# Masked attention and graph convolution over 32 items: the layer norm's steps and the last items' steps placed by hand

## The chip, the core and the metric

The kernel runs on one core of a Trainium2 chip. The metric is the device time of one execution in microseconds (us); before the change it is 2993.8 us, the median of three runs (2991.41 to 2994.5).

## The reference

32 items of 512 nodes with 512 features pass through masked attention with a layer norm, and then through a graph convolution with a layer norm. All arrays are fp32.

```python
q, k, v = (x @ Wq + bq), (x @ Wk + bk), (x @ Wv + bv)        # 8 heads of 64
scores = einsum('bihd,bjhd->bhij', q, k) / 8 + where(adj == 0, -1e9, 0)
x = layernorm(x + einsum('bhij,bjhd->bihd', softmax(scores), v))
norm_adj = adj * deg_inv_sqrt[:, None] * deg_inv_sqrt[None, :]
x = layernorm(x + einsum('nm,bmo->bno', norm_adj, x @ weight) + bias)
```

## The kernel before, in words

**Tiles and products.** Every item is a 512 x 512 matrix. The products with Wv, Wk, Wq and the convolution's weight are split into two by two blocks of 256 and done as seven block products instead of eight (`seven`, L252, and `second`, L590). For that, each weight (`wv`, `wk`, `wq`, `w1`) and the transposed input (`XT`) lies in a tile of seven slots: four blocks and three differences of them. One such product fills one PSUM buffer of the pool `ps_mm`, which has three (L91), so each product can start only when what reads the product three buffers earlier is done. Piece k of `seven` says who reads its product: k = 0 ScalarE (or VectorE, for the values), k = 1 to 6 VectorE. k = 3 is the one that makes `u2`.

**Blocks of attention.** An item's eight heads go in four blocks of two heads. `for k in range(S + 1)` (L686) runs over all 128 blocks of all items (S is 128). In a turn it makes the first half of the scores of block k (`scores`: TensorE, then VectorE's clip and mask, then ScalarE's exponential), the products with the values of block k - 1 (`values`), on every other turn the sums of the exponentials (`sums`), GpSimd's sums over tiles (`accumulate`), and the second half of the scores. Then comes a share of `side`, other work that fills TensorE.

**What sets the order.** Every engine keeps the order in which the program records its instructions (`InOrder`, L34; that is why nearly all rows of the profile have the line L44). `side` is a list of pieces (cost, function, arguments), and `run(side, share)` (L654) takes pieces from its head until their costs reach a share of the rest: a quarter in the first turn of an item, then a third, then a half, then all. A product costs 2.1, the transpose of sums 0.6, and nearly everything else 0. A piece of no cost that stands behind the product at which the share is reached waits for the next turn, behind that turn's attention.

**What side holds.** In item b's turns: the products of values, keys and queries of item b + 1 (`values_of`, `keys_and_queries`, 21 products), the transpose of item b + 2 (`turns`), the attention's layer norm of item b - 1 (`finish`, L448), and the convolution of item b - 1 (`convolve`, L546). `finish` has these steps: `inverse` (transpose of sums and reciprocals), `add` (VectorE multiplies, GpSimd adds the residual), `measure` (VectorE mean and variance), `root` (GpSimd), `judge` (a count for the fallback), `norm` (ScalarE, `hi`), `split` (VectorE `lo`, GpSimd adds the bias), `grow` (ScalarE). Each is done for four row tiles. `convolve` has four products with the adjacency (`first`), four differences (`parts`, GpSimd), seven products with the weight (`second`), and `measure`, `root` and `store`. Before the change, `weave(chain, main[5:])` (L537) spreads the 23 steps of the layer norm evenly over the products that remain.

**The end.** With no later item's products left, the last item's turns take what was held back: the `second` of item 29 (`held`) and all of item 30's convolution but its `second`. After the last turn, item 30's `second` is laid between the steps of item 31's layer norm, and item 31's own convolution follows (`block` in place of `first`, so that it can begin with the first row tile). The residuals of item 31 are loaded into two tiles of the pool `kq`, the exponentials' sums of its blocks into `acc` tiles, parts of `XT` and one `kq` tile, and its attention output into a third use of the two `yT` tiles, which item 29's convolution still reads.

Of the kernel before, what the change touches and what calls it, by code (L numbers as in the profile page):

```python
# [9 lines left out]
F32 = mybir.dt.float32  # L10
# [7 lines left out]
P = 128  # L18
# [31 lines left out]
def unshifted(  # L50
# [29 lines left out]
    B, N, D = x.shape  # L80
    NT = N // P
    DT = D // P
    G = H // 2
# [17 lines left out]
    HALF = N // 2  # L101
# [29 lines left out]
    R = {}  # L131

    def load_residual(b):

        if b < B - 2:
            t = acts.tile([P, NT, D], F32, name="xr", tag="zT", bufs=1)
            R[b] = [t[:, i, :] for i in range(NT)]
        elif b == B - 2:
            R[b] = [XT[:, i].rearrange("p u o -> p (u o)") for i in range(NT)]
        else:  # L140
            t = [acts.tile([P, 2, D], F32, name="xr2", tag="kq", bufs=5) for _ in range(2)]
            R[b] = [t[i // 2][:, i % 2, :] for i in range(NT)]
        for i in range(NT):
            nc.sync.dma_start(R[b][i], x[b, ts(i, P), :])

# [209 lines left out]
    def accumulate(s):  # L355


        b, g, jj = s
        n = 2 * ORDER.index(g) + jj
        a = None  # L360
        if b == B - 1:
            if n in (2, 6, 7):
                a = XT[:, 0:2] if n == 7 else XT[:, 4:6]
                a = a.rearrange("p k u o -> p k (u o)")
            elif n == 3:
                a = acts.tile([P, 2, N], F32, name="acc3", tag="kq", bufs=5)
        if a is None and (jj == 0 or b == B - 1):
            a = work.tile([P, 2, N], F32, name="acc", bufs=2)
        if a is not None:
            ACC.setdefault((b, g), []).append(a)  # L370
            gpsimd.tensor_add(a, E[s][0], E[s][1])
        else:
            for l in range(2):
                gpsimd.tensor_add(ACC[b, g][0], ACC[b, g][0], E[s][l])

    def values(s):

        b, g, jj = s
        e = E.pop(s)
        if jj == 0:  # L380
            AV[b, g] = ps_av.tile([P, N], F32, name="av")
        av = AV[b, g]
        for l in range(2):
            j = 2 * jj + l
            for k in range(2):
                tensor.matmul(
                    av[k * HD : (k + 1) * HD, :], V[b][:, j, ts(2 * g + k, HD)], e[l][:, k, :],
                    start=j == 0, stop=j == NT - 1,
                )
        if jj == 0:  # L390
            return

        yb = work.tile([P, 4, NT, 32], F32, name="yb", bufs=1)
        vector.transpose(
            yb.rearrange("p l i s -> p i l s"), av.rearrange("p (i r l) -> p i l r", i=NT, l=4)
        )
        if g == ORDER[0]:
            YT[b] = acts.tile([P, NT, D], F32, name="yT")  # L400
        for q in range(4):
            nc.sync.dma_start(
                YT[b][:, :, (4 * g + q) * 32 : (4 * g + q + 1) * 32],
                yb[32 * q : 32 * (q + 1)],
            )
# [131 lines left out]
    def weave(side, main):  # L537

        out, done = [], 0
        for k, piece in enumerate(main):  # L540
            due = len(side) * (k + 1) // len(main)
            out += side[done:due] + [piece]
            done = due
        return out + side[done:]

    def convolve(b):  # L546
# [22 lines left out]

        def take(d, p, copy):  # L570
            if d == 0:
                t["z"] = acts.tile([P, 4, 2, HALF], F32, name="zT", bufs=1)
            i, u = divmod(d, 2)
            z = t["z"].rearrange("p (j i) u n -> p j i u n", i=2)
            copy(z[:, :, i, u], p.rearrange("p (j n) -> p j n", j=2))
# [3 lines left out]

        def combine(at):  # L580
            if at == 0:
                t["parts"] = acts.tile([P, 3, 2, HALF], F32, name="parts", tag="hi", bufs=1)
            to, a, c = ((4, 2, 0), (5, 3, 4), (6, 3, 2), (2, 5, 1))[at]
            engine = vector if last and at < 2 else gpsimd
            engine.tensor_tensor(slot(to), slot(a), slot(c), ALU.subtract)
# [100 lines left out]
    for k in range(S + 1):  # L686
        b, at = divmod(k, G)
        if at == 1:
            run(side)
            if b:  # L690
                load_residual(b - 1)
            if b + 2 < B:
                load_x(b + 2, 0)
            if b + 1 < B:
                main, kq = values_of(b + 1) + keys_and_queries(b + 1, 0), keys_and_queries(b + 1, 1)
                turn0, turn1 = turns(b + 2) if b + 2 < B else ([], [])
                main += kq[:2] + turn0 + kq[2:5]
            if b == 0:
                w1_parts = [(0, weigh_part, (w1, gpsimd, i)) for i in range(4)]
                side = main[:7] + [(0, degrees, ())] + weave(w1_parts, main[7:]) + kq[5:] + turn1  # L700
            elif b < B - 1:
                f, c = finish(b - 1), convolve(b - 1)
                norm, split, grow = f["norm"], f["split"], f["grow"]
                chain = f["inverse"] + f["add"] + f["measure"] + f["root"] + f["judge"] + norm[:2] + split[:1]
                chain += norm[2:3] + split[1:2] + norm[3:] + split[2:] + grow
                side = weave(rest, main[:5]) + weave(chain, main[5:])
                side += c["first"] + c["parts"][:2] + kq[5:6] + c["parts"][2:3] + kq[6:] + turn1[:1]
                if b < B - 2:
                    s = c["second"]
                    side += s[:1] + c["parts"][3:] + s[1:3] + turn1[1:2] + s[3:4] + turn1[2:3] + s[4:5] + turn1[3:4]  # L710
                    side += s[5:6] + c["measure"][:1] + turn1[4:] + s[6:] + c["measure"][1:2]
                    rest = c["measure"][2:] + c["root"] + c["store"]
                else:
                    side += c["parts"][3:]
                    held = c
            else:
                f, c = finish(b - 1), convolve(b - 1)
                s, norm, split = held["second"], f["norm"], f["split"]
                side = s[:1] + f["inverse"] + s[1:2] + f["add"][:2] + s[2:3] + f["add"][2:] + s[3:4] + f["measure"][:2]
                side += s[4:5] + f["measure"][2:] + f["root"] + s[5:6] + f["judge"] + held["measure"][:2] + s[6:]  # L720
                spread = norm[:2] + held["measure"][2:3] + split[:1] + norm[2:3] + held["measure"][3:] + split[1:2]
                spread += held["root"] + norm[3:] + split[2:] + held["store"]
                side += [(0.5, *piece[1:]) for piece in spread] + c["first"] + c["parts"] + f["grow"]


        if k < S:
            scores((*blocks[k], 0))
        if k:
            values((*blocks[k - 1], 0))
            values((*blocks[k - 1], 1))  # L730
            if k % 2 == 0:
                sums(blocks[k - 1][0], (k - 1) % G // 2)
        if k < S:
            accumulate((*blocks[k], 0))
            scores((*blocks[k], 1))
            accumulate((*blocks[k], 1))
        if k == 0:
            run(two)
        if k == S - 2:
            load_residual(B - 1)  # L740
            last = finish(B - 1)
        if k == S - 1:
            run(last["early"])
        run(side, 1.0 / (G - (at - 1) % G))

    f, e = last, convolve(B - 1)
    s, norm, split, block, add = c["second"], f["norm"], f["split"], e["block"], f["late"][1:]
    run(s[:2] + f["late"][:1] + add[:2] + s[2:3] + add[2:] + s[3:4] + f["measure"] + f["root"] + s[4:5])
    run(norm[:2] + s[5:6] + split[:1] + block[:1] + norm[2:3] + split[1:2] + s[6:] + block[1:2])
    run(norm[3:] + split[2:3] + block[2:3] + split[3:] + block[3:] + f["judge"])  # L750

# [8 lines left out]
    vector.tensor_add(count, count, more)  # L762
    vector.memset(ones, 1.0)

    run(e["unload"] + e["parts"] + f["grow"])
    s, tail = e["second"], c["measure"] + c["root"] + c["store"]
    run(s[:1] + tail[:1] + s[1:2] + tail[1:2] + s[2:3] + tail[2:3] + s[3:4] + tail[3:5] + s[4:5])
    p = ps_mm.tile([1, 1], F32, name="mm")
    tensor.matmul(p, count, ones, start=True, stop=True)
    vector.tensor_scalar(bad, p, -1.0, float(P * B * NT * H + N), op0=ALU.mult, op1=ALU.add)  # L770
    run(s[5:6] + e["measure"][:2] + e["roots"][:1] + tail[5:7] + s[6:] + e["measure"][2:] + e["roots"][1:])
    run(e["stores"][:2] + tail[7:] + e["stores"][2:])
    return nc.values_load(bad, min_val=0, max_val=P * B * NT * H + N * N + N)


# [280 lines left out]
```

## Time and profile before

| what | before |
|---|---|
| median of three runs | 2993.8 us |
| span of the profiled execution | 2990.2 us |
| TensorE busy | 2880.3 us, 96% |
| VectorE busy | 1982.2 us, 66% |
| GpSimd busy | 1807.1 us, 60% |
| ScalarE busy | 1062.9 us, 36% |
| DMA, of 16 engines' span on the main queue | 19.6% |

The page names engines PE (TensorE's matmuls), PEld (its weight loads), DVE (VectorE), ACT (ScalarE), POOL (GpSimd) and SP (the engine that issues most transfers). In a row of the timeline the first number is the start in us, the second the length, "x4" how many instructions were merged into the row, and the bracket at the end the idle time ahead of it with the instruction that ended it. An fp32 matmul of the program shows as two records, so one block product of four matmuls of 256 columns shows as eight records, for keys and queries as a row of 4 with wk and one of 4 with wq. The length of a product is read from one start to the next: 1.73 us without a stall (for instance the key products at 1446.11 and 1447.84).

### The profile page before, as it was taken

How to read it: one execution, taken by the hardware profiler on the slowest of the kernel's cores; microseconds unless marked ns; L12 is line 12 of the kernel's file. 1: busy time of each engine (PE TensorE's matmuls, PEld its weight loads, DVE VectorE, ACT ScalarE, POOL GpSimd, SP SyncE). 2: the span in 40 equal slices, each digit the busy share in tenths (PEclk: the TensorE clock that was granted, in tenths of full speed). 3: DMA queues.
4: the chain of work that ended last, by engine and by line, in shares of the span. 5: the costliest groups of instructions: out<-in, count | busy, mean ns of one | idle time of the engine just before them, and what ended most of it. 6: DMA issues, size and time to landing. Idle time of an engine off the chain costs nothing. (4 is left out here: it accounts for less than half of the span.)

```text
span 2990.2 us, 35412 instructions
## 1 busy us (share of the span) xinstructions
PE 2880.3 (96%) x12966; PEld 1879.2 (63%) x12966; DVE 1982.2 (66%) x2908; ACT 1062.9 (36%) x1342; POOL 1807.1 (60%) x1141
## 2 busy tenths in 40 slices
PE   7999999999999999999999999999999999999987
PEld 5666666666666666666666666666666666666644
DVE  7666766666666667666666666676666766666765
ACT  1234323343333343333433333433334333333333
POOL 3655666656666556666566665566665666655654
PEclk9999999999999999999999999999999999999998
DMA  5111222112121112221121211122211212111111
GB/s 130 29 25 46 50 53 53 39 38 51 46 56 40 39 46 50 53 53 39 36 54 46 55 41 39 46 49 54 53 40 36 53 46 54 43 39 46 46 39 47
DMA packets 383398, 142.40 MB, mean 48 GB/s; under 512 B 280048, under 2 KB 349680, under 8 KB 383216
## 3 DMA queue, kind: packets, MB, share of 16 engines
q1 hardware_dynamic: 381920, 138.75, 19.6%
q8 instruction: 104, 1.70, 0.3%
q10 hardware_dynamic: 1296, 1.31, 0.2%
q14 instruction: 78, 0.64, 0.1%
HBM read 72.88 MB, written 33.55 MB: 36 GB/s over the span
## 5 line engine op out<-in xcount | busy, mean ns | idle before, releaser
L44 ACT ACTIVATE e<-e 128x1024 f32<-128x1024 f32 x512 | 541.2, 1057 | 1056.5 <-DVE e L44 966.2
L44 POOL TENSOR_TENSOR acc<-acc,e 128x1024 f32<-128x1024 f32 x248 | 620.0, 2500 | 158.1 <-ACT e L44 148.2
L44 DVE SCALAR_TENSOR_TENSOR e<-sc,maskT 128x1024 f32<-128x1024 f32 x512 | 601.9, 1217 | 120.3 <-PE sc L44 120.2
L44 POOL TENSOR_TENSOR acc<-e 128x1024 f32<-128x1024 f32 x129 | 303.3, 2351 | 557.9 <-PE mm L44 312.4
L44 PE MATMUL sc<-kq 64*128 64x512 f32 x2048 | 511.1, 617 | 7.9 <-DVE e L44 7.9
L44 PE MATMUL mm<-xT,wk 128*128 128x256 f32 x1792 | 472.9, 387 | 31.7 <-DVE u L44 29.5
L44 PE MATMUL av<-e,v 128*64 128x512 f32 x2048 | 469.8, 601 | 0.0
L44 PE MATMUL mm<-xT,wq 128*128 128x256 f32 x1792 | 459.9, 379 | 0.0
L44 PEld LDWEIGHTS mm<-xT,wk 128*128 128x128 f32 x1792 | 330.5, 190 | 153.9 <-issue 69.0
L44 PE MATMUL mm<-wv,xT 128*128 128x256 f32 x1792 | 402.8, 382 | 15.3 <-DMA wv<-in_L_gnn_Wv_dram 9.4
L44 PEld LDWEIGHTS mm<-wv,xT 128*128 128x128 f32 x1792 | 336.7, 191 | 83.5 <-issue 26.6
L44 PEld LDWEIGHTS mm<-xT,wq 128*128 128x128 f32 x1792 | 341.0, 190 | 45.4
L44 PEld LDWEIGHTS sc<-kq 64*128 64x128 f32 x2048 | 176.8, 186 | 278.1 <-issue 213.2
L44 PEld LDWEIGHTS av<-e,v 128*64 128x64 f32 x2048 | 136.1, 137 | 317.8 <-issue 315.7
L44 POOL TENSOR_TENSOR yT<-yT,xr 128x512 f32<-128x512 f32 (+1 forms) x128 | 180.7, 1431 | 137.4 <-DVE yT L44 128.5
L44 DVE STREAM_TRANSPOSE yb<-av 128x512 f32<-128x512 f32 x128 | 91.7, 717 | 224.9 <-PE av L44 217.2
L44 DVE TENSOR_TENSOR kq<-u,mm 128x512 f32<-128x512 f32 x128 | 87.7, 685 | 220.7 <-PE mm L44 217.1
L44 PE MATMUL mm<-w,zT 128*128 128x256 f32 x1024 | 232.4, 380 | 0.6 <-DVE zT L44 0.6
L44 POOL TENSOR_TENSOR yT<-yT,b_r 128x512 f32<-128x512 f32 x128 | 163.6, 1288 | 100.2 <-DVE lo L44 99.5
L44 PEld LDWEIGHTS mm<-w,zT 128*128 128x128 f32 x1024 | 194.3, 190 | 28.7 <-issue 1.5
L44 PE MATMUL mm<-adjT,hi 128*128 128x512 f32 x496 | 200.4, 404 | 7.6 <-DVE e L44 7.6
L44 PE MATMUL mm<-adjT,lo 128*128 128x512 f32 x496 | 197.6, 398 | 8.3 <-DVE lo L44 8.3
(103 smaller groups left out, 3044.9 us busy)
## 6 DMA issues: line engine op xcount, KB each, us to landing
x<-in_x_dram SPq DMA_DIRECT2D x256, 128.0 KB, 2.9
yT<-yb SPq DMA_DIRECT2D x512, 64.0 KB, 2.4
out_dram<-y SPq DMA_DIRECT2D x128, 256.0 KB, 2.1
xr<-in_x_dram SPq DMA_DIRECT2D x124, 256.0 KB, 3.6
wv<-in_L_gnn_Wv_dram ACTq DMA_DIRECT2D x8, 128.0 KB, 4.7
wk<-in_L_gnn_Wk_dram SPq DMA_DIRECT2D x8, 128.0 KB, 4.1
wq<-in_L_gnn_Wq_dram SPq DMA_DIRECT2D x8, 128.0 KB, 4.7
yT<-in_adj_dram SPq DMA_DIRECT2D x1, 1024.0 KB, 6.7
```

The source lines that it names most:

```text
L44: return self.tc.keep_in_program_order(op(*args, **kwargs))
```

## The change

It moves steps and changes where tiles of the last items lie. It adds no arithmetic and takes none away.

- **Middle items.** `weave` for the layer norm is replaced by a table `beside`, which names for each product of `main` by its number what follows it: the previous convolution's `measure`, `root` and `store` beside products 0 to 7, `inverse` after product 5 (it was between products 4 and 5), two `add` after 6 and two after 7, `measure` after 9, 10 and 11, `judge` after 12, `norm` and `split` after 13 to 17, and the transpose of item b + 2 after 18 (it was after 15). All four `parts` and all four `grow` follow `first`, ahead of the last two key products; two of the `parts` came after them, and `grow` was in the chain before `first`. It is there to keep a step of the layer norm from being held by the attention between two turns.
- **Last turns.** A dictionary `ending` names what each of the last turns takes: three, two and two of the seven held products of item 29 with item 30's layer norm between them. Item 30's four `first` products go behind the last turn, between the steps of item 31's layer norm, and its `second` is spread over those steps, with two products kept for the time of `unload`.
- **Tiles of the last items.** Item 31's residuals go to four slots of `wk`, its sums to pairs of slots of `wq`, `wk`, `wv` and `XT`, its attention output to `wv`, its `zT` and `parts` to `XT`: all are tiles that no later product reads. Its residuals are loaded at the start of turn S - 2 instead of the end.

```diff
-        elif b == B - 2:
-            R[b] = [XT[:, i].rearrange("p u o -> p (u o)") for i in range(NT)]
         else:
-            t = [acts.tile([P, 2, D], F32, name="xr2", tag="kq", bufs=5) for _ in range(2)]
-            R[b] = [t[i // 2][:, i % 2, :] for i in range(NT)]
+            t = XT if b == B - 2 else wk
+            R[b] = [t[:, i].rearrange("p u o -> p (u o)") for i in range(NT)]
...
-            if n in (2, 6, 7):
-                a = XT[:, 0:2] if n == 7 else XT[:, 4:6]
-                a = a.rearrange("p k u o -> p k (u o)")
-            elif n == 3:
-                a = acts.tile([P, 2, N], F32, name="acc3", tag="kq", bufs=5)
+            if n > 1:
+                t, at = ((wq, 0), (wq, 2), (wq, 4), (wk, 4), (wv, 4), (XT, 4))[n - 2]
+                a = t[:, at : at + 2].rearrange("p k u o -> p k (u o)")
...
-            YT[b] = acts.tile([P, NT, D], F32, name="yT")
+            if b < B - 1:
+                YT[b] = acts.tile([P, NT, D], F32, name="yT")
+            else:
+                YT[b] = wv[:, :NT].rearrange("p k u o -> p k (u o)")
...
-                main += kq[:2] + turn0 + kq[2:5]
+                main += kq[:5]
...
-                chain = f["inverse"] + f["add"] + f["measure"] + f["root"] + f["judge"] + norm[:2] + split[:1]
-                chain += norm[2:3] + split[1:2] + norm[3:] + split[2:] + grow
-                side = weave(rest, main[:5]) + weave(chain, main[5:])
-                side += c["first"] + c["parts"][:2] + kq[5:6] + c["parts"][2:3] + kq[6:] + turn1[:1]
+                beside = {
+                    0: rest[:1], 1: rest[1:2], 2: rest[2:3], 4: rest[3:4], 5: rest[4:5] + f["inverse"],
+                    6: rest[5:6] + add[:2], 7: rest[6:] + add[2:], 9: measure[:2], 10: measure[2:3],
+                    11: measure[3:] + f["root"], 12: f["judge"], 13: norm[:2], 14: norm[2:3] + split[:1],
+                    15: norm[3:] + split[1:2], 16: split[2:3], 17: split[3:], 18: turn0,
+                }
+                side = sum(([piece] + beside.get(i, []) for i, piece in enumerate(main)), [])
+                side += c["first"] + c["parts"] + grow + kq[5:] + turn1[:1]
...
+                ending = {
+                    S - 3: s[:1] + f["inverse"] + s[1:2] + add[:2] + s[2:3] + add[2:],
+                    S - 2: s[3:4] + f["measure"][:2] + s[6:] + f["measure"][2:] + f["root"] + f["judge"],
+                    S - 1: s[4:5] + norm[:3] + split[:1] + s[5:6] + norm[3:] + split[1:],
+                    S: [],
+                }
...
-    run(s[:2] + f["late"][:1] + add[:2] + s[2:3] + add[2:] + s[3:4] + f["measure"] + f["root"] + s[4:5])
-    run(norm[:2] + s[5:6] + split[:1] + block[:1] + norm[2:3] + split[1:2] + s[6:] + block[1:2])
-    run(norm[3:] + split[2:3] + block[2:3] + split[3:] + block[3:] + f["judge"])
+    run(first[:1] + end["late"][:1] + add[:2] + first[1:2] + add[2:] + first[2:3] + end["measure"][:2] + first[3:])
+    run(end["measure"][2:] + end["root"] + c["parts"] + f["grow"] + held["measure"] + s[:1] + norm[:1] + s[1:2])
+    run(norm[1:2] + split[:1] + s[2:3] + block[:1] + norm[2:3] + split[1:2] + s[3:4] + block[1:2] + norm[3:])
+    run(split[2:3] + s[4:5] + block[2:3] + split[3:] + block[3:] + e["unload"] + e["parts"] + s[5:] + end["grow"])
```

More of the change, by code (lines that the diff above doesn't have):

```diff
@@ L571, in take @@
             if d == 0:
-                t["z"] = acts.tile([P, 4, 2, HALF], F32, name="zT", bufs=1)
+                t["z"] = XT[:, :4] if last else acts.tile([P, 4, 2, HALF], F32, name="zT", bufs=1)
             i, u = divmod(d, 2)
@@ L581, in combine @@
             if at == 0:
-                t["parts"] = acts.tile([P, 3, 2, HALF], F32, name="parts", tag="hi", bufs=1)
+                t["parts"] = XT[:, 4:] if last else acts.tile([P, 3, 2, HALF], F32, name="parts", tag="hi", bufs=1)
             to, a, c = ((4, 2, 0), (5, 3, 4), (6, 3, 2), (2, 5, 1))[at]
@@ L696, in unshifted @@
                 turn0, turn1 = turns(b + 2) if b + 2 < B else ([], [])
-                main += kq[:2] + turn0 + kq[2:5]
+                main += kq[:5]
             if b == 0:
                 w1_parts = [(0, weigh_part, (w1, gpsimd, i)) for i in range(4)]
-                side = main[:7] + [(0, degrees, ())] + weave(w1_parts, main[7:]) + kq[5:] + turn1
+                side = main[:7] + [(0, degrees, ())] + weave(w1_parts, main[7:]) + turn0 + kq[5:] + turn1
             elif b < B - 1:
@@ L703, in unshifted @@
                 norm, split, grow = f["norm"], f["split"], f["grow"]
-                chain = f["inverse"] + f["add"] + f["measure"] + f["root"] + f["judge"] + norm[:2] + split[:1]
-                chain += norm[2:3] + split[1:2] + norm[3:] + split[2:] + grow
-                side = weave(rest, main[:5]) + weave(chain, main[5:])
-                side += c["first"] + c["parts"][:2] + kq[5:6] + c["parts"][2:3] + kq[6:] + turn1[:1]
+                add, measure = f["add"], f["measure"]
+                beside = {
[6 more added lines that the diff above has]
+                side += c["first"] + c["parts"] + grow + kq[5:] + turn1[:1]
                 if b < B - 2:
                     s = c["second"]
-                    side += s[:1] + c["parts"][3:] + s[1:3] + turn1[1:2] + s[3:4] + turn1[2:3] + s[4:5] + turn1[3:4]
+                    side += s[:1] + turn1[1:2] + s[1:4] + turn1[2:3] + s[4:5] + turn1[3:4]
                     side += s[5:6] + c["measure"][:1] + turn1[4:] + s[6:] + c["measure"][1:2]
@@ L713, in unshifted @@
                 else:
-                    side += c["parts"][3:]
                     held = c
@@ L717, in unshifted @@
                 f, c = finish(b - 1), convolve(b - 1)
[L718 to L723, printed above, removed]
+                s, norm, split, add = held["second"], f["norm"], f["split"], f["add"]
+                ending = {
[4 more added lines that the diff above has]
+                }
+        if k == S - 2:
+            load_residual(B - 1)
         if k < S:
@@ L738, in unshifted @@
             run(two)
-        if k == S - 2:
-            load_residual(B - 1)
+        if k >= S - 3:
+            run(ending[k])
+        else:
+            run(side, 1.0 / (G - (at - 1) % G))
+        if k == S - 1:
             last = finish(B - 1)
-        if k == S - 1:
             run(last["early"])
-        run(side, 1.0 / (G - (at - 1) % G))
-    f, e = last, convolve(B - 1)
-    s, norm, split, block, add = c["second"], f["norm"], f["split"], e["block"], f["late"][1:]
-    run(s[:2] + f["late"][:1] + add[:2] + s[2:3] + add[2:] + s[3:4] + f["measure"] + f["root"] + s[4:5])
-    run(norm[:2] + s[5:6] + split[:1] + block[:1] + norm[2:3] + split[1:2] + s[6:] + block[1:2])
-    run(norm[3:] + split[2:3] + block[2:3] + split[3:] + block[3:] + f["judge"])
+    end, e = last, convolve(B - 1)
+    s, first, norm, split, block, add = c["second"], c["first"], end["norm"], end["split"], e["block"], end["late"][1:]
+    run(first[:1] + end["late"][:1] + add[:2] + first[1:2] + add[2:] + first[2:3] + end["measure"][:2] + first[3:])
+    run(end["measure"][2:] + end["root"] + c["parts"] + f["grow"] + held["measure"] + s[:1] + norm[:1] + s[1:2])
+    run(norm[1:2] + split[:1] + s[2:3] + block[:1] + norm[2:3] + split[1:2] + s[3:4] + block[1:2] + norm[3:])
+    run(split[2:3] + s[4:5] + block[2:3] + split[3:] + block[3:] + e["unload"] + e["parts"] + s[5:] + end["grow"])
+    run(held["root"] + end["judge"])
     count = small.tile([P, 1], F32, name="count")
@@ L763, in unshifted @@
     vector.memset(ones, 1.0)
-    run(e["unload"] + e["parts"] + f["grow"])
     s, tail = e["second"], c["measure"] + c["root"] + c["store"]
-    run(s[:1] + tail[:1] + s[1:2] + tail[1:2] + s[2:3] + tail[2:3] + s[3:4] + tail[3:5] + s[4:5])
+    run(held["store"] + s[:1] + tail[:1] + s[1:2] + tail[1:2] + s[2:3] + tail[2:3] + s[3:4] + tail[3:5] + s[4:5])
     p = ps_mm.tile([1, 1], F32, name="mm")
@@ L771, in unshifted @@
     run(s[5:6] + e["measure"][:2] + e["roots"][:1] + tail[5:7] + s[6:] + e["measure"][2:] + e["roots"][1:])
-    run(e["stores"][:2] + tail[7:] + e["stores"][2:])
+    run(tail[7:] + e["stores"])
     return nc.values_load(bad, min_val=0, max_val=P * B * NT * H + N * N + N)
```

## The prediction

> **What bounds the kernel now.** I read the page's first part, then TensorE's row of the waits, then a timeline of one item and of the end. TensorE is the bound:
>
> ```profile
> PE 2880.3 (96%) x12966; PEld 1879.2 (63%) x12966; DVE 1982.2 (66%) x2908; ACT 1062.9 (36%) x1342; POOL 1807.1 (60%) x1141
> ```
>
> No other engine is near full, so a gain must come out of TensorE's gaps. All waits of TensorE of some size:
>
> ```profile
> PE mm L44 <- DVE u L44: 29.5, 29, 1.0
> PE mm L44 <- POOL parts L44: 20.4, 29, 1.0
> PE mm L44 <- DVE e L44: 12.2, 32, 2.0
> ...
> PE mm L44 <- DVE lo L44: 8.3, 3, 6.5
> PE sc L44 <- DVE e L44: 7.9, 3, 4.8
> PE sc L44 <- ACT hi L44: 5.4, 1, 5.4
> ```
>
> Three occur once per middle item (29 times); the last three belong to the end. In the timeline the key products start at the same offset of every item, 91.5 us apart (1362.71 to 1454.21 for the one below), so one item stands for all. Its longest gap:
>
> ```profile
> 1446.06 5.16 POOL L44 TENSOR_TENSOR acc<-acc,e 128x1024 f32<-128x1024 f32 x2 [1.14 <-ACT e L44]
> ...
> 1451.17 1.28 POOL L44 TENSOR_TENSOR yT<-yT,xr 128x512 f32<-128x512 f32 x1
> ...
> 1452.48 0.69 DVE L44 BATCH_NORM_STATS2 st<-yT 128x6 f32<-128x512 f32 x1 [2.30 <-POOL yT L44]
> ...
> 1453.31 0.84 DVE L44 SCALAR_TENSOR_TENSOR u<-e,step,mm 128x256 f32<-128x256 f32 x2
> ...
> 1454.21 1.13 PE L44 MATMUL mm<-xT,wk 128*128 128x256 f32 x4 [1.03 <-DVE u L44]
> ```
>
> The fourth `add` fell behind the next turn's `acc` on GpSimd, the fourth `measure` waits for it, and `u` (piece k = 3) stands behind `measure` on VectorE. Only `u` frees the PSUM buffer that TensorE needs. From start to start it costs more than the bracket: the four records before took 2.06 us (1452.15 to 1454.21) where 0.86 is usual, so 1.20 us. In the same way the third `second` product, waiting for a difference that GpSimd makes too late, costs 0.85 (1404.31 to 1406.89, 2.58 for 1.73), and the first adjacency product, waiting for an `e` behind `split`, 0.54 (1471.42 to 1473.05, 1.63 for 1.09). Sum 2.59 us of 91.5.
>
> The end: 2864.53, where turn S - 3 begins, to 2978.79, where the last product ends, is 114.3 us. Work in it at its own pace: 6 halves of scores at 1.92, 4 value blocks at 3.59, 2 sums at 1.87, 3 transposes at 0.44, 21 `second` products at 1.73, 8 adjacency products at 1.87: 82.2. So 32 us are lost, here:
>
> ```profile
> 2887.75 22.58 SPq L402 DMA_DIRECT2D yT<-yb  x12
> ...
> 2892.30 0.72 DVE L44 STREAM_TRANSPOSE yb<-av 128x512 f32<-128x512 f32 x1 [7.78 <-DMA yT<-yb]
> ...
> 2905.96 3.78 PE L44 MATMUL sc<-kq 64*128 64x512 f32 x8 [4.81 <-DVE e L44]
> ...
> 2917.39 0.80 PE L44 MATMUL mm<-adjT,lo 128*128 128x512 f32 x1 [6.52 <-DVE lo L44]
> ...
> 2923.23 5.71 PE L44 MATMUL av<-e,v 128*64 128x512 f32 x16
> ```
>
> Item 31's output may not land in `yT` before GpSimd has read item 29's (the queue waited 11.8 us for it), the single `yb` buffer stays full, VectorE stands 7.78 us, and all of item 30's norm is late. After each gap TensorE is slow: 5.71 us for values that take 3.65 elsewhere.
>
> **What the Trainium skill says.** "Perfetto Trace Analysis", section Optimization Strategy: the same bubble repeating on the engine that should be full can mean that no buffer was free for the next tile; the 29 equal gaps agree. "SBUF — State Buffer", section Who interferes with whom: a VectorE instruction with two SBUF inputs and a GpSimd instruction that reads SBUF exclude each other for the whole instruction. The trace agrees: two VectorE multiplies that stand beside `acc` took 3.45 us (below), 1.29 without. "TensorE: Matmul & The Clock Gate", section What's actually happening: after an idle window of about 3.4 us the array runs at half clock until busy for as long; the slow rows after 4.81 and 6.52 us agree, gaps of 1 us show none.
>
> **The change, part by part, middle items.** Products, attention and `side`'s costs are as before (the order of the changed program shows eight products in the first turn, `v` 0 to 6 and one key product, then eight, then three with four adjacency products and one key product, then one and seven).
> (a) The `e` wait. `norm` and `split` of tiles 0 to 2 now start before the turn, and `e` follows `split` 1 directly, so it needs nothing late: -0.54. ScalarE's `hi` 3 (two instructions, 0.80 + 0.72) follows the exponentials at about the old place and is needed only by the fourth row tile, 1.4 us into the product.
> (b) The `parts` wait. Four differences of 1.27 us begin as `first` ends and GpSimd's next `acc` comes 8.5 us later (1480.35 to 1488.81): 5.1 us fit, `acc` isn't moved: -0.85. `grow` now follows the four copies on ScalarE, which idles there before the exponential at 1484.53.
> (c) The `u` wait. Here the table is not what it seems: the share of the first turn is reached at product 7, so the two `add` named beside it fall behind the turn's attention. Before, that was one. Item 30 shows what two of them do, since in it two already stand there:
>
> ```profile
> 2816.62 3.45 DVE L44 TENSOR_TENSOR yT<-yT,inv 128x512 f32<-128x512 f32 x2
> ...
> 2816.81 5.48 POOL L44 TENSOR_TENSOR acc<-acc,e 128x1024 f32<-128x1024 f32 x2 [1.14 <-ACT e L44]
> ```
>
> The second multiply is shut out by `acc`. In the item above they would run from 1445.88 to 1449.33, the key product's first reader then to 1449.93. TensorE wants that buffer at 1449.56: a new stall of 0.43, with 0.1 for the restart 0.53. After it: `e` to 1450.53, two `measure` at 0.82 each to 1452.1, `u` to 1452.9 (TensorE wants it at 1453.55), `measure` 2 just as GpSimd's `add` ends (1446.06 + 5.48 + 1.28 = 1452.8), the readers of product 11 to 1454.95 (wanted 1455.28), those of 12 to 1456.5 (wanted 1457.0). So `u` no longer waits: -1.20 + 0.53.
> (d) ScalarE has `norm` 0 and 1 (about 3 us from 1457.3) before it reads the second key group's first product; VectorE's reader behind that ends at 1461.8, then comes the mask of the next scores. That is 3.1 us behind the start of these scores on TensorE (1458.75), where today it is 1.9; the first mask ends 1.2 later, and TensorE needs that buffer again 5.5 us behind the start, after 1.92 of scores and 3.59 of values. Hidden, with 1.2 us to spare.
> Sum: 2.59 - 0.53 = 2.06 us in 29 items: -60 us. Items 0 and 30: nothing (0.5 either way).
>
> **The end.** `wv` as output tile and `wk` as residual tile free the queue, so the 7.78 us wait and what follows go. Turns from 2864.53 as zero: three products in S - 3 bring S - 2 to 13.1 (was 15.2). In S - 2 the `y` sums of held product 6 wait on VectorE for GpSimd, which makes two `acc` first (to 27.4, then 2 x 1.27), with two `measure`, `root` and `judge` behind: the next mask begins at 33.0, TensorE's next half of scores at 34.3 instead of 31.3, a new gap of 3.0. Behind the last turn, VectorE has four `split` and eight half multiplies (4.92 us for eight in before, beside GpSimd) before it turns the last values: the second transpose of sums comes at 51.8 instead of 47.7, a gap of 4.1. Then item 31's `measure` and `root` end at 63.1, GpSimd makes the first two `parts` only behind them, to 65.7, and the third `second` product could start at 61.2: a gap of 4.5. The slow clock after the two longer gaps: half speed for 3.4 us, 1.7 each. With 0.8 for small ones, 15.8 + 82.2 = 98.0 instead of 114.3: -16 us. What follows the last product (11.4 us) is the same code. Bounds: -5, should every gap be twice as long, and -32 with none.
>
> Forecast: 2993.8 - 60 - 16 = 2918 us.
>
> **Rivals.**
> Full gain: the two multiplies meet `acc` less (bound: stall 0), and the end has half its gaps. 29 x 2.59 + 24 = 99: 2895 us. For: VectorE is 66% busy. Against: item 30's row.
> A wait in place of the one removed: the 0.53 delays the next readers, and product 14 waits for the readers of product 11 behind `measure` 2. My slack there is 0.3 us. If 0.8 comes back, 29 x 1.2 + 12 = 47: 2947 us. For: item 30 shows 1.17 us of waiting (2825.09) in this stretch. Against: there `e` stood behind the waiting `measure`; in the new order it doesn't.
> Slower: (d)'s slack is wrong and each turn's mask comes too late, so that TensorE waits for scores. It takes more than 76 / 29 = 2.6 us per item; at 3.3 it is 29 x 3.3 - 76 = +20: 3014 us. Against: 1.2 us of slack in (d), and exponentials that TensorE wants a turn later.
>
> **How the numbers follow.** Forecast 0.62, full gain 0.15, wait in its place 0.15, slower 0.08. Range 2890 to 2952: both neighbours are in it. Faster by over 0.2% 0.90, the same 0.02, slower 0.08.
>
> **What would show it.** Right: 89.4 us between items; no row of TensorE waiting for `u` or `parts` in middle items; a wait of about 0.4 for the first `kq` reader; no wait for `yT`'s transfer near the end; `yT` multiplies in pairs of 3.4 us. Wrong: a new row of TensorE's waits with 29 entries of over 1 us, or scores that wait for VectorE's `e`.

## The result and the profile after

| | median | against before |
|---|---|---|
| before | 2992.95 us | |
| after | 2956.01 us (2954.46 to 2957.25) | 0.9876 [0.9859, 0.9893] |

Both medians are of four runs; the 2993.8 given earlier is that of the first three of the kernel before. The change gains 37 us, 1.2%. The direction was forecast, the size was not: 2918 was predicted, and 2956 lies above the range of 2890 to 2952. The first part of the page of the changed kernel:

```profile
PE 2872.4 (97%) x12966; PEld 1878.3 (64%) x12966; DVE 2057.9 (70%) x2908; ACT 1062.3 (36%) x1342; POOL 1819.9 (62%) x1141
```

VectorE has the same 2908 instructions and is busy 76 us longer (1982.2 before). That is the first sign: instructions that do the same work have become longer. TensorE's waits in the changed kernel (total us, times, longest):

```profile
PE mm L44 <- DVE lo L44: 25.2, 30, 1.1
PE mm L44 <- DVE xT L44: 11.5, 2, 9.2
PE mm L44 <- DVE kq L44: 10.4, 30, 3.0
PE sc L44 <- DVE e L44: 6.4, 4, 2.8
PE mm L44 <- DVE sT L44: 5.1, 1, 5.1
...
PE mm L44 <- POOL parts L44: 3.1, 1, 3.1
PE mm L44 <- DVE y L44: 2.5, 1, 2.5
```

The rows for `u` (29 times) and `parts` (29 times) are gone, and `e` no longer stands there 32 times. Two rows with 30 entries took their place. `kq` was forecast, and `lo` was not. (`xT` is at the start of the program, and so is one of the two longest waits of `sc` for `e`.) Items are now 90.35 us apart, 91.47 before: 29 x 1.12 = 32.5 us.

Both rows in the timeline of one item of the changed kernel, first the stall that was forecast, then the one that was not:

```profile
1431.35 3.45 DVE L44 TENSOR_TENSOR yT<-yT,inv 128x512 f32<-128x512 f32 x2
1431.54 5.48 POOL L44 TENSOR_TENSOR acc<-acc,e 128x1024 f32<-128x1024 f32 x2 [1.14 <-ACT e L44]
...
1434.73 0.67 DVE L44 TENSOR_TENSOR kq<-e,mm 128x512 f32<-128x512 f32 x1
1435.46 1.13 PE L44 MATMUL mm<-xT,wk 128*128 128x256 f32 x4 [0.26 <-DVE kq L44]
...
1444.59 0.75 DVE L44 SCALAR_TENSOR_TENSOR lo<-yT,dis,hi 128x512 fp32r<-128x512 f32 x1 [1.22 <-ACT hi L44]
...
1453.27 0.74 DVE L44 SCALAR_TENSOR_TENSOR lo<-yT,dis,hi 128x512 fp32r<-128x512 f32 x1
1453.46 5.58 POOL L44 TENSOR_TENSOR acc<-acc,e 128x1024 f32<-128x1024 f32 x2 [0.20 <-ACT e L44]
...
1454.53 2.26 DVE L44 SCALAR_TENSOR_TENSOR lo<-yT,dis,hi 128x512 fp32r<-128x512 f32 x1
1455.18 0.72 ACT L44 ACTIVATE hi<-yT,dis 128x512 fp32r<-128x512 f32 x1
...
1457.50 2.09 DVE L44 SCALAR_TENSOR_TENSOR lo<-yT,dis,hi 128x512 fp32r<-128x512 f32 x1
...
1459.64 0.50 PE L44 MATMUL mm<-adjT,lo 128*128 128x512 f32 x1 [0.83 <-DVE lo L44]
```

The two multiplies take 3.45 us beside `acc`, as forecast; the records before the waiting product took 1.29 us (1434.17 to 1435.46) where 0.865 is usual, and its own start 0.1 more: 0.52 us. The first `lo` of the item stands ahead of the next turn's attention (1444.59). The other three fall behind it: the second starts just before `acc` and takes 0.74, and the last two stand beside `acc` and take 2.26 and 2.09. The first `acc` ends at about 1456.25 (1453.46 + half of 5.58) and the third `lo` 0.5 later, the second `acc` at 1459.04 and the last `lo` 0.5 later. The fourth `hi` was done at 1455.90, so ScalarE isn't what holds it. The record before the waiting adjacency product took 1.23 (1458.41 to 1459.64) where 0.23 is usual: with 0.1 for the restart, 1.1 us.

Before the change only two of the four `lo` fell behind the turn, and they missed most of `acc`. This is the kernel before:

```profile
1458.70 1.19 DVE L44 SCALAR_TENSOR_TENSOR lo<-yT,dis,hi 128x512 fp32r<-128x512 f32 x1 [0.71 <-ACT hi L44]
...
1468.53 0.74 DVE L44 SCALAR_TENSOR_TENSOR lo<-yT,dis,hi 128x512 fp32r<-128x512 f32 x1
1468.72 5.59 POOL L44 TENSOR_TENSOR acc<-acc,e 128x1024 f32<-128x1024 f32 x2 [1.37 <-ACT e L44]
...
1471.20 0.85 DVE L44 SCALAR_TENSOR_TENSOR lo<-yT,dis,hi 128x512 fp32r<-128x512 f32 x1 [0.77 <-ACT hi L44]
```

The third started just ahead of the first `acc`, the fourth 0.3 us before the end of it. In the changed kernel the second `lo` has taken the place ahead of `acc`, and the third and the fourth are pushed into it.

Item 30 has a longer `kq` wait of its own, here in its timeline (changed kernel):

```profile
2784.96 7.87 DVE L44 TENSOR_TENSOR yT<-yT,inv 128x512 f32<-128x512 f32 x4
...
2793.48 1.32 PE L44 MATMUL mm<-xT,wk 128*128 128x256 f32 x4 [2.95 <-DVE kq L44]
2794.60 1.91 PE L44 MATMUL mm<-xT,wq 128*128 128x256 f32 x4
2796.30 1.72 PE L44 MATMUL mm<-xT,wk 128*128 128x256 f32 x4
```

It has fewer pieces left, so its first share ends at product 6 and all four multiplies fall behind the turn. From its transpose of sums to turn S - 3 it takes 66.3 us (2772.68 to 2839.00); before it took 61.9, and with the transpose one product later it should be 60.2. So 6.1 us are lost.

From turn S - 3 (2839.00) to the end of the last product (2942.2) it is 103.2 us instead of 114.3, so 11 gained. The gaps that are left there:

```profile
2873.77 2.26 PE L44 MATMUL sc<-kq 64*128 64x512 f32 x8 [2.83 <-DVE e L44]
...
2886.28 5.22 DVE L44 TENSOR_TENSOR wv<-wv,inv 128x128 f32<-128x128 f32 x8
...
2892.76 1.11 PE L44 MATMUL mm<-ident,sT 128*128 128x128 f32 x4 [5.11 <-DVE sT L44]
...
2907.36 3.45 PE L44 MATMUL mm<-w,parts 128*128 128x256 f32 x8 [3.10 <-POOL parts L44]
...
2928.80 2.93 ACT L44 ACTIVATE y<-y,add,rstd 128x512 f32<-128x512 f32 x4 [3.82 <-POOL add L44]
...
2931.64 0.56 ACT L44 COPY e<-mm 128x512 f32<-128x512 f32 x1
...
2933.07 5.38 PE L44 MATMUL mm<-w,xT 128*128 128x256 f32 x16 [2.52 <-DVE y L44]
```

The first three were forecast by place (3.0, 4.1 and 4.5 us). The fourth was not: item 29's last normalization stands on ScalarE ahead of the copy that frees TensorE's buffer, and waits for GpSimd's `add`.

So 32.5 - 6.1 + 11.1 = 37.5 us, of the 37 measured.

### The profile page after: what moved, and what is told of

It reads as the page before. It is cut to its first block, busy times and chain, and to the rows that moved or that the text cites. A ratio compares the mean times of both kernels' runs of the same rounds, so it can differ in the third digit from the quotient of the medians.

```text
span 2953.2 us, 35448 instructions
## 1 busy us (share of the span) xinstructions
PE 2872.4 (97%) x12966; PEld 1878.3 (64%) x12966; DVE 2057.9 (70%) x2908; ACT 1062.3 (36%) x1342; POOL 1819.9 (62%) x1141
## 4 chain that ended last, share of the span: by engine, by line
PE 80%; DVE 15%; issue 4%; DMA 1%; ACT 0%; POOL 0%; SPq 0%; DVEq 0%; POOLq 0%; ACTq 0%
PE mm L44 50%; PE av L44 15%; PE sc L44 15%; DVE e L44 5%; DVE yT L44 3%; DVE lo L44 3%; DVE u L44 1%; DVE kq L44 1%; DMA x<-in_x_dram 0%; DVE xT L44 0%; DVE wv L44 0%; DVE st L44 0%; DVE y L44 0%; ACT yT L44 0%; ACT hi L44 0%
## 5 line engine op out<-in xcount | busy, mean ns | idle before, releaser
L44 POOL TENSOR_TENSOR acc<-acc,e 128x1024 f32<-128x1024 f32 x248 | 628.5, 2534 | 126.0 <-ACT e L44 116.1
L44 POOL TENSOR_TENSOR acc<-e 128x1024 f32<-128x1024 f32 x126 | 296.6, 2354 | 517.3 <-ACT e L44 273.8
L44 POOL TENSOR_TENSOR yT<-yT,xr 128x512 f32<-128x512 f32 x120 | 161.7, 1368 | 179.2 <-DVE yT L44 173.0
L44 PE MATMUL mm<-w,zT 128*128 128x256 f32 x992 | 224.8, 379 | 0.0
L44 POOL TENSOR_TENSOR yT<-yT,b_r 128x512 f32<-128x512 f32 x124 | 170.9, 1399 | 75.4 <-DVE lo L44 75.4
L44 DVE SCALAR_TENSOR_TENSOR lo<-yT,dis,hi 128x512 fp32r<-128x512 f32 x124 | 181.5, 1464 | 39.8 <-ACT hi L44 39.8
L44 PEld LDWEIGHTS mm<-w,zT 128*128 128x128 f32 x992 | 188.2, 190 | 27.1 <-issue 1.5
```

The source lines that it names most:

```text
L44: return self.tc.keep_in_program_order(op(*args, **kwargs))
```

## The experiments

The theory: the missing gain of the middle items is the lateness of `lo`, which waits for GpSimd's `acc`; item 30's four multiplies and the `y` wait of the end are the rest. All edits are on the changed kernel, except the first two.

### The two parts apart

`e1_middle_only` has the new table of the middle items and the last items as before; `e2_end_only` the reverse.

```diff
 # e1_middle_only: the kernel before, with
-                main += kq[:2] + turn0 + kq[2:5]
+                main += kq[:5]
...
+                beside = { ... }
 # e2_end_only: the kernel before, with
+                ending = { ... }
...
+            if n > 1:
+                t, at = ((wq, 0), (wq, 2), (wq, 4), (wk, 4), (wv, 4), (XT, 4))[n - 2]
```

> Only the middle items' part of the change (the table beside the products, parts and grow ahead, the transpose later); last turns, end and tiles of the last items as before. If the two parts add up, the new waits of 1.1 us for lo and 0.43 + 0.1 for kq leave 2.59 - 1.7 = 0.9 us per item: 29 x 0.9 = 26 below the kernel before, about 2967 us. If the shorter end of the changed kernel is in truth caused by the middle items (their work handed on earlier), this run has nearly all of the 37 us: about 2957.

> Only the last turns, the end and the tiles of the last items as in the changed kernel; middle items as before. If the parts add up: 114.3 - 103.2 = 11 us below the kernel before, about 2982. If the end gains only together with the middle part: about 2993.

Measured: 2967.0 us, 0.9912 [0.9895, 0.9928], with items 90.36 us apart; and 2981.85 us, 0.9964 [0.9951, 0.9976]. The gains of 26 and 11 add up to the 37 of the whole: the parts don't disturb each other by more than about a microsecond, and each can be explained by itself.

### Without the sums beside `lo`

This kernel leaves out two of GpSimd's sums in the fourth block of items 1 to 30, the ones that stand beside `split`.

```diff
-            for l in range(2):
+            for l in range(2 if ORDER.index(g) != 3 or not 0 < b < B - 1 else 0):
```

> The changed kernel without GpSimd's two sums of the second half in the fourth block of items 1 to 30 (this block's sums of exponentials then lack half of their terms; everything else is computed). Theory, exclusion: lo 2 and lo 3 last 2.1 to 2.3 us because VectorE reads two SBUF inputs while GpSimd makes those sums. Then lo falls to 0.75 us, TensorE's wait for lo goes, 29 x 1.1 = 32 less: about 2924. Rival, lateness: lo 3 is late because ScalarE makes the fourth hi behind the turn's exponentials; then the wait of 0.83 stays and the time is about 2956.

Measured: 2924.84 us, 0.9771 [0.9754, 0.9787]. The waits hold no row for `lo`; `kq` is as it was:

```profile
PE mm L44 <- DVE kq L44: 10.4, 30, 3.0
```

The mean length of `lo` fell from 1464 to 1027 ns (before the change it was 901). Items are 89.27 us apart, 1.08 less: 29 x 1.08 = 31 us, the whole difference. ScalarE makes the fourth `hi` 10.6 us behind the first `lo` in both kernels (1431.45 to 1442.05 here, 1444.59 to 1455.18 with the sums), so its lateness, the rival, isn't the cause. Without GpSimd's sums beside it `lo` isn't late, though it still takes longer than alone: GpSimd's additions of the bias now stand beside it.

### Without the sums beside `add`

The same one block earlier: two sums of the third block of items 1 to 30 are left out.

```diff
-            for l in range(2):
+            for l in range(2 if ORDER.index(g) != 2 or not 0 < b < B - 1 else 0):
```

> The changed kernel without the two sums of the second half in the third block of items 1 to 30, beside which the last two multiplies of add stand (these sums of exponentials lack half of their terms). Exclusion: the two multiplies fall from 3.45 to about 1.3 us and the wait for kq (0.26 in the waits, 0.53 from start to start) goes: 29 x 0.5 = 15 less, about 2941; the wait for lo stays, since that is in another turn. Lateness (VectorE simply has too much in this stretch): kq's wait stays, about 2956.

Measured: 2935.39 us, 0.981 [0.9793, 0.9826]. No row of `kq` is left, a pair of multiplies takes 1.28 us, and the other wait stands untouched:

```profile
PE mm L44 <- DVE lo L44: 25.3, 30, 1.2
...
PE mm L44 <- DVE sT L44: 4.3, 1, 4.3
```

Items are 89.80 apart, 0.55 less, so 16 of the 20.6 us gained are the middle items'. The rest was not in the expectation: it is mostly item 30's, whose longest `kq` wait (3.0) is gone too. The two stalls are independent of each other, and 0.52 + 1.1 us is the right division.

### The same sums in halves

All the work is done, but each of these sums of 128x1024 goes as two of 128x512. An instruction that is shut out then waits for a shorter one.

```diff
-                gpsimd.tensor_add(ACC[b, g][0], ACC[b, g][0], E[s][l])
+                for h in range(2):
+                    a = ACC[b, g][0][:, h]
+                    gpsimd.tensor_add(a, a, E[s][l][:, h])
```

> The changed kernel with each of GpSimd's two sums of a second half (128 x 1024) as two instructions of 128 x 512; all work is done. If VectorE is shut out for one whole GpSimd instruction at a time, each wait is halved: the two multiplies from 3.45 to about 2.3 us (kq's wait goes), lo 2 and lo 3 from 2.2 to about 1.5 us (TensorE's wait for lo goes), at about 0.1 us more of GpSimd per sum. 29 x (1.1 + 0.5) = 46 less than 2956: about 2910. If VectorE has to wait until GpSimd has no instruction left to start, both sums still pass ahead: about 2956.

Measured: 2922.5 us, 0.9768 [0.9752, 0.9785]: 33.5 us below the changed kernel, 12 above what was expected. The timeline of this kernel shows the multiplies, then `lo`:

```profile
1416.85 2.37 DVE L44 TENSOR_TENSOR yT<-yT,inv 128x512 f32<-128x512 f32 x2
1417.03 5.77 POOL L44 TENSOR_TENSOR acc<-acc,e 128x512 f32<-128x512 f32 x4 [1.14 <-ACT e L44]
...
1424.06 0.69 DVE L44 BATCH_NORM_STATS2 st<-yT 128x6 f32<-128x512 f32 x1 [1.09 <-POOL yT L44]
...
1426.29 1.10 PE L44 MATMUL mm<-xT,wk 128*128 128x256 f32 x4 [0.41 <-DVE e L44]
...
1440.12 1.17 DVE L44 SCALAR_TENSOR_TENSOR lo<-yT,dis,hi 128x512 fp32r<-128x512 f32 x1
...
1441.99 0.97 DVE L44 SCALAR_TENSOR_TENSOR lo<-yT,dis,hi 128x512 fp32r<-128x512 f32 x1
```

The pair takes 2.37 us instead of 3.45, and `lo` 1.17 and 0.97 instead of 2.26 and 2.09. TensorE waits for neither in the middle items. But a new wait of 0.41 us stands in each item: the third `measure` now waits 1.09 us for GpSimd's residual sums, which begin behind the longer `acc`, and the reader `e` behind it frees TensorE's buffer late. That is the prediction's second rival, "a wait in place of the one removed", at the place that it named, but in this kernel and not in the changed one. Items are 89.35 us apart, so 0.63 us per item above the 88.72 of the kernels without any of these stalls (last experiment). That is 18 us in 29 items, more than the 12 by which the run stays behind its expectation; item 30, whose longest `kq` wait fell from 3.0 to 0.8 us, makes up for part of it.

The Trainium skill's "SBUF — State Buffer", section Who interferes with whom, says that the engine that comes second is blocked for the whole instruction of the other. Shortening that instruction shortened the wait (2.26 to 1.17 us), although GpSimd was busy longer in all, so this run agrees.

### The multiplies ahead of the turn

All four `add` stand beside product 6, so that none falls behind the turn's attention.

```diff
-                    6: rest[5:6] + add[:2], 7: rest[6:] + add[2:], 9: measure[:2], 10: measure[2:3],
+                    6: rest[5:6] + add, 7: rest[6:], 9: measure[:2], 10: measure[2:3],
```

> The changed kernel with all four add behind product 6, so that they fall ahead of the turn's attention, where the name of the change has them. Exclusion: no multiply meets GpSimd's sums, kq's wait goes as in the run without these sums (2935): 2936 to 2941. Rival: four multiplies ahead of the turn hold up the mask of its scores, and what is won is lost there: about 2956 or more.

Measured: 2940.52 us, 0.9826 [0.981, 0.9842]. Items are 89.85 us apart, 0.50 less. One `kq` wait is left, item 30's 3.0, and `lo` stays at 27.1 in 30. The stall goes when the multiplies are moved, with no sum left out: its cause is where they stand. They are hardly faster there. The four take 4.64 us, against 1.29 + 3.45 in the changed kernel, with GpSimd's additions of the residual now running beside them (1416.40 to 1422.65). What changed is that no reader that TensorE waits for stands behind them.

### Item 30's multiplies

Item 30 alone takes its four `add` behind product 5.

```diff
-                    4: rest[3:4], 5: rest[4:5] + f["inverse"],
-                    6: rest[5:6] + add[:2], 7: rest[6:] + add[2:],
+                    4: rest[3:4], 5: rest[4:5] + f["inverse"] + (add if b == B - 2 else []),
+                    6: rest[5:6] + (add[:2] if b < B - 2 else []), 7: rest[6:] + (add[2:] if b < B - 2 else []),
```

> The changed kernel with the four add of item 30's turn (the item with 25 products, whose first turn ends one product earlier) behind product 5 instead of 6 and 7, so that they run ahead of the attention. In the changed kernel these four multiplies last 7.87 us and TensorE waits 2.95 for kq and is slow behind it. Theory: 4 to 6 us less, 2950 to 2952. Rival: the last turns take up the gain, since item 31's attention sets the end: about 2956.

Measured: 2951.65 us, 0.9865 [0.9848, 0.9881], so 4.4 us less; the longest `kq` wait is 0.3. In this run's trace item 30 takes 61.4 us (2774.23 to 2835.64) instead of 66.3, so 4.9 of its 6.1 us are the multiplies. Its `lo` wait (1.1 with the restart) stays, and that is the rest.

### The end with three waits taken out

A held product that nothing reads late takes the place of product 6 in turn S - 2; two `parts` go ahead of `root`; item 29's `store` goes behind item 31's first products.

```diff
-                    S - 2: s[3:4] + f["measure"][:2] + s[6:] + f["measure"][2:] + f["root"] + f["judge"],
-                    S - 1: s[4:5] + norm[:3] + split[:1] + s[5:6] + norm[3:] + split[1:],
+                    S - 2: s[3:4] + f["measure"][:2] + s[4:5] + f["measure"][2:] + f["root"] + f["judge"],
+                    S - 1: s[6:] + norm[:3] + split[:1] + s[5:6] + norm[3:] + split[1:],
...
-    run(end["measure"][2:] + end["root"] + c["parts"] + f["grow"] + held["measure"] + s[:1] + norm[:1] + s[1:2])
+    run(end["measure"][2:] + c["parts"][:2] + end["root"] + c["parts"][2:] + f["grow"] + held["measure"] + s[:1] + norm[:1] + s[1:2])
...
-    run(held["store"] + s[:1] + tail[:1] + s[1:2] + tail[1:2] + ...)
+    run(s[:1] + held["store"][:2] + tail[:1] + s[1:2] + held["store"][2:] + tail[1:2] + ...)
```

> The changed kernel with four moves in the last turns and the end: held product 4 in place of 6 in turn S - 2 (its y sum needs no GpSimd work behind the turn's sums), the first two parts ahead of item 31's root, item 29's stores behind the first products of the last convolution. Takes the waits of 2.83 (scores for e), 3.10 (parts) and 2.52 (y behind ScalarE's stores): 8.5 less, and up to 1.7 more where the slow clock behind a gap goes: 2946 to 2948. If the chain of item 31's layer norm behind the 5.11 us wait for sT sets the end whatever fills TensorE: no gain, 2956.

Measured: 2948.2 us, 0.9851 [0.9834, 0.9867]: 7.8 us less. The rows for `parts` and `y` are gone from TensorE's waits, the one of scores for `e` fell from 6.4 to 3.5 (the 2.8 left in it is at the start of the program), and that for `sT` stays at 5.1. A new one of 1.8 us appears (scores for `lo`, once).

### Everything together

`e8_halves_and_end` is the halves with the end's moves. `e10_together` adds the multiplies ahead of the turn, item 30's too. `e11_together_yb` also moves the eight half multiplies of item 31 that stood 5.22 us long ahead of the last `sT`:

```diff
-            run(last["early"])
+            run(last["early"][:1])
+        if k == S:
+            run(last["early"][1:])
```

> Both the sums in halves and the four moves in the end, over the changed kernel; all work is done. If the two are independent, their gains add: 2956 - 46 - 10 = 2900. If the end takes up what the middle gains or the other way round: about 2910.

> Sums in halves, the four moves in the end, and all add ahead of the attention (behind product 6, for item 30 behind product 5); all work is done. The wait of 0.41 us for e that is left per item in the run with halves (product 11's readers behind a measure that waits for GpSimd's add) goes: 29 x 0.45 = 13, and some 2 in item 30, less than 2914.6: about 2899. If the add ahead bring new waits of the mask, as much comes back: about 2914.

> The run before with item 31's eight half multiplies behind the turn of its last values on VectorE instead of ahead of it. The wait of 5.1 us for sT at the end goes and the transfer of the last output starts 4 us earlier: about 4 us less, 2895. If VectorE's whole chain (the eight multiplies included) sets the measure of item 31, nothing comes of it: about 2899.

Measured:

- `e8_halves_and_end`: 2914.58 us, 0.974 [0.9723, 0.9756]. This is where the two measured gains add (33.5 + 7.8). It misses its 2900 mostly because the wait of the halves for `e`, 15.3 us in 31, isn't touched by the end.
- `e10_together`: 2895.36 us, 0.9675 [0.9659, 0.9691], 19 us less, where about 15 were expected. The wait for `e` is gone too: with the multiplies ahead of the turn GpSimd adds the residuals early.
- `e11_together_yb`: 2891.27 us, 0.9666 [0.965, 0.9682], 4.1 us less, as expected, and the row for `sT` is gone.

The whole list of TensorE's waits of the last kernel down to 1.7 us:

```profile
PE mm L44 <- DVE xT L44: 10.3, 2, 9.3
PE sc L44 <- DVE e L44: 3.6, 3, 2.8
PE mm L44 <- DVE e L44: 2.0, 1, 2.0
PE sc L44 <- DVE lo L44: 1.8, 1, 1.8
PE mm L44 <- POOL parts L44: 1.7, 1, 1.7
```

No row has an entry per item any more, and between 1000 and 1180 us, two items, the list is empty. Items are 88.72 us apart. That is the pace of TensorE without stalls, and it measures what the stalls cost: 91.47 - 88.72 = 2.75 us per item before, 90.35 - 88.72 = 1.63 after (0.52 for `kq`, 1.1 for `lo`). This kernel computes everything and is 65 us below the changed one, 101 below the one before.

## Why the prediction was wrong

| term | predicted | measured |
|---|---|---|
| waits removed, per middle item | -2.59 us | -2.75 us |
| new `kq` stall, per item | +0.53 us | +0.52 us |
| new `lo` stall, per item | 0 | +1.1 us |
| 29 items | -60 us | -32.5 us |
| item 30 | 0 | +6 us |
| the end | -16 us | -11 us |
| sum | -76 us | -37.5 us |

**Right.** The three removed waits, by place and size. (c)'s new stall: multiplies of 3.45 us beside `acc`, and 0.52 us at the first `kq` reader; it goes with the sums and with the move. (b), with no row of `parts` left in middle items, and (d): no scores wait for the mask in middle items. In the end the three gaps stand where they were put, and the 7.78 us wait for the transfer is gone. Their sum of 11.0 us (2.83 + 5.11 + 3.10) against 11.6 is in part luck: the second came out 1.0 us longer than forecast (4.1) and the third 1.4 shorter (4.5).

**The step that failed** is (a), "so it needs nothing late: -0.54", which put the wait for `lo` at nothing. Two things were wrong in it.

- The place. "`norm` and `split` of tiles 0 to 2 now start before the turn" holds for `norm`, and of `split` for tile 0 alone. The second turn takes eight products, by the prediction's own count, so its share is reached at product 15, and the `split` named beside 15 falls behind the turn's attention, as the two `add` beside product 7 do in (c). The second `lo` starts 8.7 us behind the first (1444.59, 1453.27), where it was 1.5 before (1457.24, 1458.70). So the change put three `lo` behind the turn instead of two, not one.
- The cost. The rule of (c), two inputs in SBUF beside GpSimd's `acc`, was applied to the multiplies and not to `lo`, which reads `yT` and `hi`, both in SBUF. Two waits of up to a whole `acc` made the last `lo` 1 us too late for the fourth row tile, in every item: 29 x 1.1 = 32 us, of which the run without those sums gives back 31.

(a) followed ScalarE's fourth `hi` ("needed only by the fourth row tile"), which was right and not the question. "Hidden, with 1.2 us to spare" covered (d)'s mask alone; no slack was computed for `lo`. That the stall needs the sums is shown; whether it would also go with the second `lo` moved ahead of the turn was not tried.

**"Items 0 and 30: nothing"** failed for item 30. The prediction had read how two multiplies look there, but took the share's end for middle items (product 7) only. With item 30's shorter list it comes at product 6, all four multiplies fall behind the turn, and 6 us are lost; 4.4 come back when they are moved.

**The end** was right in mechanism and off in size: 5 us. The `y` wait of 2.52 us was not seen, and the sixteen records behind it took 5.4 us where 3.5 is usual (0.216 each), so 1.9 more; the granted clock was 0.5 for 3.4 us there (2934.24 to 2937.65). Less the 0.6 by which the three forecast gaps were shorter, that is 3.8 of the 5; the rest lies in small gaps that were not followed one by one.

The mechanism of the second rival (2947) did not occur in the changed kernel: no product waits for a reader behind `measure` in the middle items. That its number lies nearer to the 2956 measured is chance.

## What to carry to other kernels

When steps are moved by hand, take each VectorE instruction with two SBUF inputs at its new place and look at what GpSimd runs there; here one such instruction after another lost up to a whole GpSimd instruction each, and what waits behind the last one decides whether it costs anything. Where they must meet, try GpSimd's instruction in halves: here it cost GpSimd 0.3 to 0.8 us per four halves and took 1.1 us off each wait. In a list cut by shares of cost, what is named beside the last product of a share falls behind the next turn: here two `add` (product 7) and a `split` (product 15). A shorter list has its cuts elsewhere, so the first and last items have to be followed by themselves.

## What was not expected of the hardware

- An excluded instruction is booked as busy, not as waiting: `lo` has a mean of 1464 ns after and 901 before, and VectorE's busy time rises by 76 us with the same 2908 instructions. No wait ahead of a `lo` is put down to GpSimd. The sign is a longer mean for the same shape.
- GpSimd pays less than VectorE. Two sums take 4.81 us where no multiply stands beside them (`e7_adds_ahead`), 5.48 beside two multiplies and 5.58 beside `lo`; as four halves 5.77 and 6.33.
- TensorE went to half speed after a gap of 2.95 us (item 30: eight records in 3.3 us, 2794.60 to 2797.86, where 1.73 is usual), but not after one of 2.83 (2873.77: eight records in 2.19, then the usual pace). The granted clock in the traces tells the two apart. It was 0.5 from 2794.29 to 2797.71, and in each trace it changes only at the edges of equal steps of 3.41 us. Of the first gap 2.60 us fell into one step; an edge cut the second into 1.86 and 0.97. In `e9_item30_adds` the gap ahead of the same scores (2.82 us) had 2.65 in one step and was followed by 0.5. Over all thirteen traces, each of the 40 steps at full clock in which TensorE had no matmul running for 2.0 us or more was followed by a step at 0.5, and no such step with less than 1.8 us was. So a gap of this length costs up to 1.7 us more (half of 3.41) or nothing, by where it falls. The Trainium skill's "TensorE: Matmul & The Clock Gate", section What's actually happening, has an idle window of about 3.4 us; the length of the step agrees, but 2.0 us without matmuls inside it were enough here.
